# The order around a state-space scan: layer-norm steps one unit earlier, up-projection copies one unit later, one z projection moved

## The chip, the cores and the metric

The kernel runs on one core of a Trainium2 chip. The metric is the device time of one execution in microseconds (us); before the change it is 9294.69 us, the median of three runs that lie between 9293.85 and 9295.26 us.

A core has a matrix engine (PE), a vector engine (DVE), a scalar/activation engine (ACT), a general engine (POOL) and DMA queues, here nearly all fed by SP. Each engine executes its own instructions strictly in the order in which the program gives them; they wait for each other through semaphores.

## The reference: what is computed

The input is a batch of 8 feature maps of 384 channels on 32 x 32 points. Four layers follow each other, each with a group norm in front and a residual around it: a selective state-space layer, a deformable convolution, a second state-space layer with a layer norm ahead of it and a two-layer perceptron (MLP) behind it, and a displaced 5 x 5 convolution. The change touches only the third of them:

```python
def _L2_conv_ref(x, ...):                        # x is already group-normed
    t = x.transpose(0, 2, 3, 1).reshape(b, L, c) # L = 1024 tokens, c = 384
    mu = t.mean(-1, keepdims=True)
    var = t.var(-1, keepdims=True)
    t = (t - mu) * rsqrt(var + 1e-05) * ln_w + ln_b
    xz = t @ in_proj_w.T                         # 384 -> 2 x 768
    xm, z = jnp.split(xz, 2, axis=-1)
    xc = silu(causal_conv3(xm) + conv_b)
    dt, Bm, Cm = split(xc @ x_proj_w.T)
    dt = softplus(dt @ dt_proj_w.T + dt_proj_b)
    # over the 1024 tokens, for 768 channels x 16 states:
    #   h = exp(dt * A) * h + dt * xc * Bm ;  y = sum_n h * Cm
    y = (y + xc * D) * silu(z)
    t = y @ out_proj_w.T
    t = gelu(t @ mlp_w1.T + mlp_b1) @ mlp_w2.T + mlp_b2
```

## The kernel before

`ssm_layer` (called with li = 2 for this layer, where `mlp` is true) cuts the work into 16 steps: 8 samples, each in two halves of 512 tokens. A step has 48 units, written t = 0 to 47: 6 blocks of 128 channels (j) by 8 units (m). A unit is one scan instruction over 128 partitions and 2 x 512 elements. Steps of the first half of a sample are called even here, those of the second half odd. All times quoted for one step are those of step 6 (even) and step 7 (odd).

In a unit each engine has a fixed part, in this order:

- ACT: the unit's entries of the hand-written list `act[t]`, in even steps a tiny copy of the last state (L520), then the two exponentials "decays" (L494) for the scan *two units ahead*, which go into one of two PSUM buffers `da`.
- DVE: the scan (L514); in 5 of 8 units the product with C (`with_c`, L527), which in the other 3 (m = 0, 2, 5) is on POOL (L525); then the list `dve[t]`.
- POOL: the scan's inputs (L502) for three units ahead, into one of three buffers `db`; then `with_c` where it is POOL's; then `pool[t]`.
- PE: the list `pe[t]`, then, in two of 8 units, `read_out` (L537), which sums four units' products into `y` and so frees their `hs` buffers, of which there are seven.

Everything else of a step is put into these lists by `plan`: for step s it places the work of the *next* step's head (norms, in projections `inner`, convolution, x and dt projections), of the present step (z projections and gates), and of the *previous* step's tail (out projection, the MLP's up and down projections). The place in a list alone sets the order on an engine; nothing is rearranged later.

The pieces that matter here, with the line under which the trace shows them:

- the layer norm of the next step: `norm_apply` (ACT, L299), `ln_mean` (PE, L307, into `ps_mu`), `ln_center` (DVE, L312), `ln_square` (ACT, L316), `ln_var` (PE, L321, into `ps_var`), `ln_rstd` (ACT, L326 and L327), `ln_scale` (DVE, L332), `ln_affine` (ACT, L337), and then the first in projection `inner` (PE, L348, unit 16), its copy `conv_last` (ACT, L352) and `conv` (DVE, L368);
- the MLP of the previous step: in each of three rounds q four up projections `mlp_up` (PE, L595), each copied out by `up_take` (ACT, L606), then `gelu` (ACT, L609: a load of ACT's function table and one instruction), `exp_ln` (L377, a table load back), and three down projections (PE, L614) with their sums on DVE (L621, L623);
- the z projection of block 4 (PE, L546) and its gate at unit 31 (ACT, L550, with its own table load);
- of the dt path: `dt_proj` (PE, L408), `soft_exp` (ACT, L414 to L420), `soft_rest` (DVE, L427), `soft_sum` (POOL, L435 to L437), and at the end of a block `close` (DVE, L556 and L557), which reads `y`; `x_store` (ACT, L391) is the copy that dt projections of the next step wait for.

All matrix products named above, except `read_out`, take their PSUM buffer from one pool of three, in turn: the n-th product can start only when the consumer of the (n-3)-rd has read it. In units 8 to 16 the order before is: z0, z1, up 0, up 1, dt projection 3, `ps_mu`, up 2, up 3, `ps_var`, in projection 0.

```python
self.mm = ctx.enter_context(tc.tile_pool(name=f"mm{li}", bufs=3, space=PSUM))
dap = ctx.enter_context(tc.tile_pool(name=f"da{li}", bufs=1, space=PSUM))  # two tags: da0, da1
t = s["hs", m] = p2.tile([P, 2, TS], F32, name="hs", tag="hs", bufs=7)
```

Weights come by DMA ahead of use: a z projection's slice is fetched two units before it (`TZ[j] - 2`), on SP's queue, with three buffers.

Of the kernel before, what the change touches and what calls it, by code (L numbers as in the profile page):

```python
# [96 lines left out]
class Net:  # L97
# [107 lines left out]
    def ssm_layer(self, li, src, dst, shift=None):  # L205
        tc, nc, ins = self.tc, self.nc, self.ins
        mlp = li == 2
# [3 lines left out]
        with ExitStack() as ctx:  # L211
# [435 lines left out]


            TG, TS2 = ((8, 8, 24, 24, 31, 47), (24, 31)) if mlp else ((7, 15, 23, 31, 39, 47), (23, 31))
            TZ = (6, 7, 22, 23, 30, 45) if mlp else tuple(t - 1 for t in TG)  # L650
            TI = (16, 17, 18, 24, 25, 26) if mlp else (15, 16, 17, 24, 25, 26)
            NU = NS // 2
            T = ND * NU
# [1 line left out]
            def plan(prev, s, nxt):  # L655
                act, dve, pool, pe = queues = [[[] for _ in range(T + NU)] for _ in range(4)]

                def put(q, t, fn, *args):
                    if not args or args[0]:
                        q[t].append((fn, *args))  # L660

                for j in range(ND):
                    t = NU * j
                    put(dve, t + 2, close, *((s, j - 1) if j else (prev, ND - 1)))
                    tz = TZ[j]
                    put(pe, tz - 2, fetch_in, s, ND + j)
                    put(pe, tz, z_proj, s, j)
                    put(act, TG[j], gate, s, j)

                    n, k = (s, j + 2) if j + 2 < ND else (nxt, j + 2 - ND)  # L670
                    put(pe, t + 2, dt_proj, n, k)
                    put(act, t + 3, soft_exp, n, k)
                    put(dve, t + 4, soft_rest, n, k)
                    put(act, t + 5, soft_ln, n, k)
                    if pe_sum:
                        put(pe, t + 5, soft_add, n, k)
                        put(act, t + 6, soft_take, n, k)
                        put(dve, t + 7, soft_du, n, k)
                    else:
                        put(pool, t + 6, soft_sum, n, k)  # L680
                    put(pool, t + 7, spread, n, k)
                for i, t in enumerate(TS2):
                    put(act, t, silu, nxt, 3 * i, 3 * i + 3)
                for t in sorted({*TG, *TS2}):
                    put(act, t, exp_ln)
                put(pe, 0, norm_load, nxt)
                if nxt and nxt["h"] == 0:
                    put(dve, 2, norm_stats, nxt, 0)
                    put(dve, 3, norm_stats, nxt, 1)
                    put(dve, 3, lambda n: n.update(gn_mv=self.gn_aggr(n["gn_st"])), nxt)  # L690
                    put(pe, 4, lambda n: n.update(gn_ps=self.gn_mean(n["gn_mv"])), nxt)
                    put(dve, 5, lambda n: n.update(gn_grp=self.gn_dev(n["gn_mv"], n["gn_ps"])), nxt)
                    put(act, 6, lambda n: n.update(gn_dm=self.gn_square(n["gn_grp"][1])), nxt)
                    put(pe, 6, lambda n: n.update(gn_ps=self.gn_mean2(n["gn_dm"])), nxt)
                    put(dve, 8, lambda n: n.update(gn_var=self.gn_sum(n["gn_grp"][0], n["gn_ps"])), nxt)
                    put(act, 9, lambda n: n.update(gn=self.gn_rstd(n["gn_grp"][0], n["gn_var"])), nxt)
                    put(act, 9, lambda n: n["sib"].update(gn=n["gn"]), nxt)
                put(act, 10, norm_apply, nxt)
                if mlp:
                    put(pe, 10, ln_mean, nxt)  # L700
                    put(dve, 12, ln_center, nxt)
                    put(act, 13, ln_square, nxt)
                    put(pe, 13, ln_var, nxt)
                    put(act, 14, ln_rstd, nxt)
                    put(dve, 15, ln_scale, nxt)
                    put(act, 16, ln_affine, nxt)
                for d, t in enumerate(TI):
                    put(pe, t - 2, fetch_in, nxt, d)
                    put(pe, t, inner, nxt, d)
                    put(act, t + 1, conv_last, nxt, d)  # L710
                    put(dve, t + 2, conv, nxt, d)
                put(pe, 32 if mlp else 30, x_proj, nxt, 0, ND // 2)
                put(pe, 33 if mlp else 32, x_proj, nxt, ND // 2, ND)
                put(act, 34 if mlp else 33, x_store, nxt)
                for p, t in enumerate((36, 45)):
                    put(pool, t, load_bc, nxt, p)
                put(act, 7 if mlp else 9, residual, prev)
                for o, (t, e) in enumerate(((0, 2), (1, 3), (4, 5)) if mlp else ((8, 9), (10, 11), (12, 13))):
                    if mlp and o < 2:
                        put(pe, (T - 9, T - 6)[o], fetch, nxt and s, "out", o)  # L720
                    else:
                        put(pe, 0, fetch, prev, "out", o)
                    put(pe, t, out_proj, prev, o, 0, ND // 2)
                    put(pe, e, out_proj, prev, o, ND // 2, ND)
                    put(act if mlp else dve, e + (1 if mlp else 2), out_take, prev, o)
                if mlp:
                    ups = ((8, 9, 11, 12), (27, 28, 29, 31), (37, 38, 39, 40))
                    downs = ((19, 20, 21), (34, 35, 36), (43, 44, 46))
                    for q, g in enumerate((15, 33, 41)):
                        put(pe, (3, 15, 31)[q], fetch, prev, "up", q)  # L730
                        put(pe, (12, 28, 38)[q], fetch, prev, "down", q)
                        for f, t in enumerate(ups[q]):
                            put(pe, t, mlp_up, prev, q, f)
                            put(act, t + 1, up_take, prev, q, f)
                        put(act, g, gelu, prev)
                        put(act, g, exp_ln)
                        for o, t in enumerate(downs[q]):
                            put(pe, t, mlp_down, prev, q, o)
                            put(dve, min(t + 2, T - 1), down_take, prev, q, o)
                return queues  # L740
# [6 lines left out]
            with tc.manual_schedule(engines=ENGINES):  # L747
# [37 lines left out]
                for i, (s, j, m) in enumerate(units):  # L785
                    c, t = divmod(i, T)
                    if t == 0:
                        queues = plan(
                            steps[c - 1] if c else None, s, steps[c + 1] if c + 1 < len(steps) else None
                        )  # L790
                        for k, q in enumerate(over or ()):
                            for i0, items in enumerate(q):
                                queues[k][i0][:0] = items
                        act, dve, pool, pe = queues
                        over = [q[T:] for q in queues]
# [1140 lines left out]
```

## Time and profile before

| | |
|---|---|
| median of the three runs | 9294.69 us |
| the profiled execution | 9297.33 us |
| its span, first to last instruction | 9295.5 us |
| mean granted PE clock | 0.884 |
| even step, first scan to the next step's first scan (steps 2, 4, 6, 8, 10, 12, 14) | 191.3 to 191.4 us |
| odd step (3, 5, 7, 9, 11, 13) | 204.6 us |
| step 0 / step 1 | 199.1 / 199.6 us |

The step lengths are differences between starts of scans (L514) in the trace: step 6 begins at 7026.64 us, step 7 at 7217.99, step 8 at 7422.6. They repeat to about 0.1 us, so one even and one odd step stand for all. A line of the timeline gives start, duration, engine, source line, operation, what is written from what, how many instructions are merged, and in brackets how long the engine was idle before it and which instruction's end let it go. A line of the waits gives the total of such idle time, how often, and the longest. Matrix products in float32 appear as two passes each, so one of three matrix multiplications shows as x6.

### The profile page before, as it was taken

What the parts mean: (1) busy time and instruction counts of PE and PEld (TensorE: products, weight loads), DVE (VectorE), ACT (ScalarE), POOL (GpSimd) and SP (SyncE); (2) the same over time, 40 slices, a digit from 0 to 9 for tenths busy, and PEclk for the clock granted to TensorE, in tenths of its full rate; (3) what the DMA queues carried; (4) which work ended last, traced back from release to release, by engine and by line L of the source; (5) the groups of instructions that cost most, each with busy time, mean ns of one, the idle gap of its engine ahead of it and who ended that gap; (6) DMA issues with size and microseconds to landing.
All of it is one profiled execution on the core that took longest, in us unless ns stands there. A gap on an engine that the chain in (4) does not pass through costs nothing. (4 is left out here: it accounts for less than half of the span.)

```text
span 9295.5 us, 93074 instructions
## 1 busy us (share of the span) xinstructions
PE 7557.6 (81%) x29452; PEld 3856.6 (41%) x29452; DVE 7733.3 (83%) x8617; ACT 6500.3 (70%) x10467; POOL 5645.4 (61%) x3393
## 2 busy tenths in 40 slices
PE   6777677677676999999999997588888888888876
PEld 2222222222223777767777766133333333333333
DVE  6999999999995878878878877788988889898972
ACT  5677677677673878878877876677777677776750
POOL 6999999999994000000000000898989989899964
PEclk7788788788787999999999998798999889999988
DMA  4544544544543333333333333566656666666656
GB/s 123 124 115 113 123 116 114 123 119 114 123 114 81 82 80 85 92 83 85 90 84 86 91 80 85 118 154 151 150 139 155 151 161 147 148 148 145 161 145 112
DMA packets 785233, 1094.47 MB, mean 118 GB/s; under 512 B 274963, under 2 KB 427955, under 8 KB 752985
## 3 DMA queue, kind: packets, MB, share of 16 engines
q1 hardware_dynamic: 722628, 1077.98, 47.6%
q10 hardware_dynamic: 62100, 10.44, 0.7%
q8 instruction: 235, 3.85, 0.2%
q14 instruction: 270, 2.20, 0.1%
HBM read 917.84 MB, written 170.33 MB: 117 GB/s over the span
## 5 line engine op out<-in xcount | busy, mean ns | idle before, releaser
L502 POOL TENSOR_TENSOR db<-dub,bc 128x1024 f32<-128x1024 f32 x1536 | 3603.2, 2355 | 405.9 <-DVE hs L514 224.6
L494 ACT ACTIVATE da<-dtb,vec 128x512 f32<-128x512 f32 x3072 | 2119.5, 691 | 672.9 <-DVE hs L527 416.9
L514 DVE TENSOR_TENSOR_SCAN da<-da,db 128x1024 f32<-128x1024 f32 x912 | 2086.3, 2288 | 258.9 <-ACT da L494 116.4
L435 POOL TENSOR_TENSOR dt<-dt,sp_e 128x512 f32<-128x512 f32 x96 | 122.3, 1274 | 2885.4 <-DMA bc<-bcd 2881.1
L1598 PE MATMUL wacc<-fsm,fxk 128*128 128x221 f32 (+34 forms) x10624 | 1657.2, 315 | 98.1 <-DVE fsm L1568 95.1
L1598 PEld LDWEIGHTS wacc<-fsm,fxk 128*128 128x128 f32 x10624 | 1570.0, 195 | 236.1 <-DVE fsm L1568 159.2
L514 DVE TENSOR_TENSOR_SCAN hs<-da,db 128x1024 f32<-128x1024 f32 x624 | 1423.9, 2282 | 166.4 <-POOL db L487 76.7
L525 POOL TENSOR_TENSOR hs<-hs,bc 128x1024 f32<-128x1024 f32 x624 | 1470.8, 2357 | 15.2 <-ACT st L520 14.9
L1568 DVE TENSOR_TENSOR fsm<-fhy,fhx 128x170 f32<-128x170 f32 (+42 forms) x3216 | 1170.2, 428 | 342.3 <-PE wacc L1598 315.3
L527 DVE TENSOR_TENSOR hs<-da,bc 128x1024 f32<-128x1024 f32 x912 | 1116.9, 1225 | 111.8 <-PE y L537 58.5
L537 PE MATMUL y<-hs,cols 128*32 128x512 f32 x6144 | 826.1, 618 | 160.5 <-POOL hs L525 154.6
L1528 ACT ACTIVATE fhy<-fpyx,cell 128x416 f32<-128x416 f32 (+9 forms) x1280 | 645.5, 576 | 385.0 <-DVE fsm L1568 385.0
L1551 DVE TENSOR_TENSOR fxk<-fxt,fwk 128x1024 f32<-128x1024 f32 (+1 forms) x688 | 787.1, 1179 | 10.2 <-ACT fxt L1330 10.2
L614 PE MATMUL ps_m<-hid,wm 128*128 128x512 f32 x1152 | 550.2, 633 | 61.7 <-ACT hid L609 27.7
L595 PE MATMUL ps_h<-t,wm 128*128 128x512 f32 x1152 | 529.7, 604 | 43.2 <-DVE sp_e L427 25.4
L1533 ACT ACTIVATE fhy<-fhy,cols 128x1344 f32<-128x1344 f32 (+10 forms) x368 | 530.8, 1442 | 12.0
L537 PEld LDWEIGHTS y<-hs,cols 128*32 128x32 f32 x6144 | 171.3, 112 | 798.3 <-issue 497.7
L348 PE MATMUL ps_in<-xn,winr 128*128 128x512 f32 x576 | 328.9, 718 | 174.5 <-ACT xn L337 125.4
L444 PE MATMUL ps_sp<-dt,ident 128*128 128x512 f32 x192 | 168.4, 974 | 290.8 <-ACT dt L414 285.7
L614 PEld LDWEIGHTS ps_m<-hid,wm 128*128 128x128 f32 x1152 | 226.9, 203 | 394.3 <-issue 282.7
L1239 PE MATMUL ps_off<-fxn,fow 128*98 128x465 f32 (+10 forms) x896 | 386.6, 579 | 0.0
L444 PE MATMUL ps_sp<-sp_e,ident 128*128 128x512 f32 x192 | 174.9, 1009 | 259.5 <-DVE sp_e L425 259.5
(212 smaller groups left out, 10436.4 us busy)
## 6 DMA issues: line engine op xcount, KB each, us to landing
dtb<-dtd SPq DMA_DIRECT2D x768, 256.0 KB
dub<-dtd SPq DMA_DIRECT2D x768, 256.0 KB
fpyx<-fposd SPq DMA_DIRECT2D x640, 256.0 KB
wm<-in_w SPq DMA_DIRECT2D x96, 768.0 KB
bc<-bcd SPq DMA_DIRECT2D x256, 256.0 KB
x<-x SPq DMA_DIRECT2D x71, 768.0 KB
dtd<-dt SPq DMA_DIRECT2D x192, 256.0 KB
dtd<-sp_e SPq DMA_DIRECT2D x192, 256.0 KB
```

The source lines that it names most:

```text
L494: nc.scalar.activation(da[:, i, :], s["dtb", j][:, k, :], AF.Exp, scale=na[:, j, n + i : n + i + 1])
L502: nc.gpsimd.tensor_tensor(db, du, s["bc"][p][:, 0], ALU.mult)
L514: nc.vector.tensor_tensor_scan(h1, da1, db1, 0.0, ALU.mult, ALU.add)
L525: nc.gpsimd.tensor_tensor(s["hs", m], s["hs", m], c, ALU.mult)
L527: nc.vector.tensor_tensor(hs_tile(s, m), s["da", m], c, ALU.mult)
L537: nc.tensor.matmul(s["y"][k * IP : (k + 1) * IP, :], sel, s["hs", p * NSUB + k][:, i, :], start=mlp and p == 0 and i == 0, stop=p == NQP - ...
L614: nc.tensor.matmul(ps, s["w2", q][:, f, o * P : (o + 1) * P], s["hid", q][:, f, :], start=(f == 0), stop=(f == 3))
L1528: nc.scalar.activation(hy[:, at : at + (yb - ya) * W], pyx[:, 0, ya * W : yb * W], AF.Abs, bias=bias)
L1533: nc.scalar.activation(hy[:, :at], hy[:, :at], AF.Relu, bias=self.col(Q_ONE), scale=-1.0)
L1551: nc.vector.tensor_tensor(t[:, :n], x, wk[:, j : j + 1, :].to_broadcast([P, n, P]), ALU.mult)
L1568: nc.vector.tensor_tensor(self.sub(sm, at, [(r * w, n), (w, r), (1, w)]), self.sub(hy, hy_at[by] + xa, [(r * W, n), (W, r), (1, w)]), self ...
L1598: nc.tensor.matmul(a[:, ya - 4 * o : yb - 4 * o, xa:xb], k, self.sub(sm, sm_at[by], [(w, yb - ya), (1, w)]), start=False, stop=False,)
```

## The change

Nothing is added or taken away; five kinds of entries change their place in the lists.

- `ln_center` moves from unit 12 to 11, `ln_square` and `ln_var` from 13 to 12, `ln_rstd` from 14 to 13, `ln_scale` from 15 to 14, `ln_affine` from 16 to 15. `norm_apply` and `ln_mean` stay at 10.
- Each `up_take` moves one unit later, but not past the unit of its round's `gelu` (15, 33, 41).
- In round 1 the third up projection moves from unit 29 to 30.
- The z projection of block 4 moves from unit 30 to 29, and its weight fetch from 28 to 27.

```diff
-            TZ = (6, 7, 22, 23, 30, 45) if mlp else tuple(t - 1 for t in TG)
+            TZ = (6, 7, 22, 23, 29, 45) if mlp else tuple(t - 1 for t in TG)
...
                 put(act, 10, norm_apply, nxt)
                 if mlp:
                     put(pe, 10, ln_mean, nxt)
-                    put(dve, 12, ln_center, nxt)
-                    put(act, 13, ln_square, nxt)
-                    put(pe, 13, ln_var, nxt)
-                    put(act, 14, ln_rstd, nxt)
-                    put(dve, 15, ln_scale, nxt)
-                    put(act, 16, ln_affine, nxt)
+                    put(dve, 11, ln_center, nxt)
+                    put(act, 12, ln_square, nxt)
+                    put(pe, 12, ln_var, nxt)
+                    put(act, 13, ln_rstd, nxt)
+                    put(dve, 14, ln_scale, nxt)
+                    put(act, 15, ln_affine, nxt)
...
                 if mlp:
-                    ups = ((8, 9, 11, 12), (27, 28, 29, 31), (37, 38, 39, 40))
+                    ups = ((8, 9, 11, 12), (27, 28, 30, 31), (37, 38, 39, 40))
                     downs = ((19, 20, 21), (34, 35, 36), (43, 44, 46))
                     for q, g in enumerate((15, 33, 41)):
...
                         for f, t in enumerate(ups[q]):
                             put(pe, t, mlp_up, prev, q, f)
-                            put(act, t + 1, up_take, prev, q, f)
+                            put(act, min(t + 2, g), up_take, prev, q, f)
                         put(act, g, gelu, prev)
                         put(act, g, exp_ln)
```

In units 9 to 16 the lists read, before and after:

| unit | before | after |
|---|---|---|
| 9 | ACT: up_take 0 | |
| 10 | ACT: norm_apply, up_take 1. PE: dt projection 3, ln_mean | ACT: norm_apply, up_take 0. PE: the same |
| 11 | ACT: soft_exp 3. PE: up 2 | ACT: soft_exp 3, up_take 1. DVE: ln_center. PE: up 2 |
| 12 | ACT: up_take 2. DVE: soft_rest 3, ln_center. PE: up 3 | ACT: ln_square. DVE: soft_rest 3. PE: ln_var, up 3 |
| 13 | ACT: soft_ln 3, ln_square, up_take 3. PE: ln_var | ACT: soft_ln 3, ln_rstd, up_take 2 |
| 14 | ACT: ln_rstd | ACT: up_take 3. DVE: ln_scale |
| 15 | ACT: gelu, exp_ln. DVE: ln_scale | ACT: ln_affine, gelu, exp_ln |
| 16 | ACT: ln_affine. PE: in projection 0 | PE: in projection 0 |

In round 1 the copies are at units 29, 30, 32, 33 instead of 28, 29, 30, 32, with the gelu at 33; in round 2 at 39, 40, 41, 41 instead of 38, 39, 40, 41, with the gelu at 41.

## The prediction

> **What bounds the kernel now.** First the page.
>
> ```profile
> span 9295.5 us, 93074 instructions
> ...
> PE 7557.6 (81%) x29452; PEld 3856.6 (41%) x29452; DVE 7733.3 (83%) x8617; ACT 6500.3 (70%) x10467; POOL 5645.4 (61%) x3393
> ```
>
> These shares run over four layers. In the stretch from 5800 to 8990 us, the third layer, POOL is busy 2889 of 3190 us, DVE 2780, PE 2605, ACT 2273. No engine is full; what counts is what ends DVE's pauses, since a step is 48 scans in a row. The chain that ended last says nothing here: it covers only the last 180 us, in the fourth layer. So next the waits between 5900 and 8780 us (14 steps).
>
> ```profile
> DVE da L514 <- ACT da L494: 84.3, 47, 2.6
> ...
> DVE y L556 <- PE y L537: 24.4, 14, 2.0
> ...
> ACT hid L606 <- PE ps_h L595: 152.6, 98, 5.1
> ...
> PE ps_in L348 <- ACT xn L337: 121.2, 15, 8.6
> ...
> PE ps_h L595 <- DVE sp_e L427: 25.4, 27, 1.2
> ```
>
> DVE is held by late decays and, once a step, by `y`. ACT's 152.6 us for up projections and PE's 121.2 us for the normed tokens are large, but they cost only what reaches a scan. The last line proves the three-buffer rule: up 3 waits for `soft_rest` 3, the reader of the dt projection three products earlier. Then the timeline of step 6, units 10 to 18, PE first, then ACT, then DVE:
>
> ```profile
> 7062.40 5.49 PE L307 MATMUL ps_mu<-xn,mean_w 128*128 128x512 f32 x6 [2.09 <-ACT xn L299]
> ```
>
> ```profile
> 7075.01 2.84 PE L321 MATMUL ps_var<-sq,mean_w 128*128 128x512 f32 x6 [1.13 <-ACT sq L316]
> 7077.78 1.92 PE L537 MATMUL y<-hs,cols 128*32 128x512 f32 x16
> 7087.71 5.13 PE L348 MATMUL ps_in<-xn,winr 128*128 128x512 f32 x6 [8.01 <-ACT xn L337]
> ```
>
> ```profile
> 7061.55 2.21 ACT L299 ACTIVATE xn<-x,gn_nb,gn_rstd 128x512 f32<-128x512 f32 x3
> 7063.66 0.66 ACT L606 ACTIVATE hid<-ps_h,vec 128x512 f32<-128x512 f32 x1
> ```
>
> ```profile
> 7077.89 0.66 ACT L326 ACTIVATE ps_var<-ps_var,cols 128x512 f32<-128x512 f32 x1 [0.96 <-PE ps_var L321]
> ...
> 7082.09 1.91 ACT L609 ACTIVATE hid<-hid 128x2048 f32<-128x2048 f32 x1
> ...
> 7085.51 1.42 ACT L494 ACTIVATE da<-dtb,vec 128x512 f32<-128x512 f32 x2
> ```
>
> ```profile
> 7065.70 1.22 DVE L527 TENSOR_TENSOR hs<-da,bc 128x1024 f32<-128x1024 f32 x1
> ...
> 7070.90 1.87 DVE L312 TENSOR_TENSOR xn<-xn,ps_mu 128x512 f32<-128x512 f32 x3
> ```
>
> ```profile
> 7087.01 2.30 DVE L514 TENSOR_TENSOR_SCAN da<-da,db 128x1024 f32<-128x1024 f32 x1 [1.07 <-POOL sp_e L437]
> ...
> 7094.79 0.76 DVE L556 SCALAR_TENSOR_TENSOR y<-u,vec,y 128x512 f32<-128x512 f32 x1 [1.94 <-PE y L537]
> ```
>
> To see: `ps_mu` ends at 7067.9, while DVE ends unit 11's product at 7066.9; centring in unit 12 (7070.9) has 3 us to spare. The scan of unit 17 waits 1.07 us; POOL is named, but the decays it needs ended at 7086.93, behind the gelu, so ACT holds it too. `close` waits 1.94 us because PE stood 8.01 us ahead of in projection 0 with `read_out` behind it.
>
> **Part 1: the norm's steps and round 0's copies, even steps.** Today `ps_mu` needs the buffer of up 0, whose copy is in unit 9. The copy moves behind `norm_apply`. `norm_apply` begins 0.65 us earlier (7060.9 to 7063.1), the copy ends at 7063.7, and only then `ps_mu` starts: 7063.75, plus 5.49, is 7069.25. In unit 11 DVE reaches `ln_center` at 7066.92 and waits 2.35 us; behind it stand all later scans. Centring 1.87: the scan of unit 12 starts at 7071.1. From there 4.06 us (7066.84 to 7070.90 today, without centring) to the scan of unit 13: 7075.15 against 7072.69, so +2.45.
>
> `ps_var`, now ahead of up 3, inherits that product's wait for `soft_rest` 3, which ends at about 7075.2. PE has been idle since 7072.1 (up 2 behind `ps_mu`), 3.1 us. Its length is unknown: 2.84 us as in the row after 1.13 us idle, or 5.49 as after 2.09; an in projection after 2.82 idle took 4.32 (at 7132.14), a z projection after 3.50 idle 5.5. I take 4.75, between the last two: end 7079.95. Then on ACT: `ln_rstd` 1.24, copy 0.6, decays for unit 15 1.6 with the state copy: 7083.4; copy 0.6, state copy and first token 0.35, decays for unit 16 1.45: 7085.8; `ln_affine`, now ahead of the gelu, 2.15; gelu with its two table loads 4.5; state copy and decays for unit 17 1.6: 7094.05. Today the scan of unit 17 starts at 7087.01, so +7.0. From it `close` can follow 5.85 us later; today it starts 1.94 after that, which vanishes since in projection 0 starts some 8 us ahead of need. Net **+5.1 us**; with `ps_var` at 2.84 it is +3.2, at 5.49 +5.9. From unit 19 to 25 DVE has no pause that could take this up, and POOL, which idles 3 us for DVE there (unit 21), none either.
>
> The clock: that PE ran `ps_mu` at 0.86 us a pass after 2.09 us idle is the row I go by. [...]
>
> **Odd steps.** `norm_apply` 7267.6 to 7269.8, copy to 7270.4, `ps_mu` 2.84 (PE is warm there, 7270.12 today) to 7273.2; DVE is free at 7272.5, waits 0.7; the scan of unit 13 at 7279.0 against 7278.31. Up 2 waits for its buffer till 7274.8 (`soft_exp` goes ahead of the copy), `ps_var` for `soft_rest` till 7279.1, end 7281.95. Then 1.24 + 0.6 + 1.4 + 0.6 + 1.1 (`first_token` with its four exponentials) + 1.4 + 2.15 + 4.5 + 1.45 lead to 7296.4 against 7292.67: +3.8, less `close`'s wait of 1.52: **+2.3**.
>
> **Part 2: round 1 and the z projection.** From the gate in unit 31 to `x_store` ACT has no pause (7148.51 to 7164.78), and the scans of units 33 and 35 wait for it, 2.40 and 0.97 us. A copy more stands ahead of the gelu (two in units 32 and 33 instead of one): +0.6 us. The 1.26 and 0.33 us that ACT waited in units 29 and 30 vanish, but it waits 0.92 for DVE right after, so nothing is gained. The z projection trades places with up 2 on PE, both 2.8 us; up 3 ends when it did. In odd steps the gate's 0.20 us wait for it goes: +0.4. Its weight fetch meets the same neighbours on SP's queue and the same buffer condition: nothing, and no DMA is added on SP or POOL.
>
> **Part 3: round 2.** Copies leave units 38 and 39, where ACT waited 5.01 and 2.33 us; that frees the decays for unit 41 (its scan waits 1.65). But the gelu in unit 41 needs up 3 of a PE chain without a gap from 7166.84 to 7194.6, ready at 7191.7 as today. The scan of unit 43 stays where it is and waits 4.3 instead of 2.61: 0.
>
> **Sum.** Seven even steps with both neighbours: 7 x (5.1 + 0.6) = 39.9. Seven odd ones (1 to 13, step 1 taken as the rest): 7 x (2.3 + 0.4) = 18.9. Step 15 has only part 2: 0.4. Step 0 has no MLP behind it: the same `ps_mu`, 2.8 us later decays for unit 15, given back where today's product waited 1.26 and `ln_scale` stood in unit 15: 0. In all 59.2 on the profiled 9297.33 us, which lies 2.6 above the median: 9356.5, and **9354** as a median.
>
> **Rivals.**
> - The move does what the waits promise: PE no longer stands before in projection 0, the scan of unit 17 (1.07, odd 1.10) and `close` (1.94, 1.52) no longer wait. With part 2's cost: 7 x (-2.4) + 7 x (-2.2) = -32, 9262. It decides if `ps_mu` ends before DVE's unit 11 product and the decays for unit 17 before unit 16's scan ends. For it: the large PE and ACT waits. Against: `ps_mu` misses even today, by 1.0 us, and `ln_affine` adds 2.15 us in front of the gelu in either step.
> - `ps_mu` is not held by the copy, the buffer being free otherwise: DVE then waits 1.0 instead of 2.35 and PE keeps warm: even +0.5, odd +2.0, with part 2 7 x 1.1 + 7 x 2.4 = 24.5, 9319. Against: the buffers go strictly in turn, as up 3's wait shows.
> - Worse: PE goes cold in odd steps too (1.65 us idle before up 2, where 1.50 was still warm and 2.09 not), `ps_var` 2.6 later: 7 x 6.5 + 7 x 5.3 = 83, 9377.
>
> **Chances.** My forecast 0.66, worse 0.08, the small loss 0.12, the gain 0.10, about nothing (gain and loss cancelling) 0.04. 0.2%, 18.6 us, is about what can be told from no change; the small loss falls just beyond it, with a third of its chance inside. So faster 0.10, same 0.08, slower 0.82. Range 9312 to 9384: from the small loss, which a cheaper `ps_var` (9341) lies above, to the worse case and its own error of a unit's wait.
>
> **What would show it.** A wait DVE L312 on `ps_mu` of about 2.4 us (even) and 0.7 (odd); `ps_mu` starting right after a copy L606; the scan of unit 17 held by ACT by some 5 us; no wait of `close` in unit 18; PE's 8 us ahead of in projection 0 down to about 3; ACT's waits on `ps_h` nearly gone with no gain. I am wrong if `ln_center` does not wait, or if the scan of unit 17 starts less than 2 us later than now.

## The result, and the profile after

| | before | after |
|---|---|---|
| median of 13 runs each, same chip | 9295.25 us (9288.03 to 9300.62) | 9314.15 us (9308.49 to 9317.4) |
| ratio after / before, 95% interval | | 1.002 [1.0013, 1.0028] |
| profiled execution: span | 9295.5 us | 9315.6 us |
| mean granted PE clock | 0.884 | 0.885 |

The change costs 18.9 us. The direction was forecast, the size (59) was three times too large. First the page of the kernel after:

```profile
span 9315.6 us, 93049 instructions
...
PE 7571.2 (81%) x29427; PEld 3863.6 (41%) x29452; DVE 7732.7 (83%) x8617; ACT 6505.8 (70%) x10467; POOL 5648.0 (61%) x3393
```

Nothing was taken away; the 25 PE records fewer than before are matrix products that the trace lacks (the weight loads, PEld, are 29452 in both). DVE, ACT and POOL are busy as long as before to within 6 us, PE 13.6 us longer; DVE's idle time grew by 20.7 us, about the whole difference of the spans. The waits of the kernel after between 5900 and 8780 us (engine, waiting line, what it waited for; total, times, longest), DVE's first:

```profile
DVE da L514 <- ACT da L494: 100.7, 44, 3.5
...
DVE xn L312 <- PE ps_mu L307: 14.0, 13, 1.4
...
DVE y L556 <- PE y L537: 7.4, 13, 0.7
```

```profile
ACT hid L606 <- PE ps_h L595: 32.8, 33, 1.9
```

```profile
PE ps_in L348 <- ACT xn L337: 47.8, 15, 3.5
...
PE ps_mu L307 <- ACT hid L606: 26.9, 14, 3.5
...
PE ps_var L321 <- ACT sq L316: 6.9, 7, 1.0
```

ACT's wait for up projections fell by 120 us and PE's for the normed tokens by 73, and the kernel is slower, so neither wait was what set its time. `ps_mu` now waits for the copy of up 0, DVE for `ps_mu`, and the decays come later. The last line is the one that the prediction did not have: `ps_var` waits for ACT's square, and no wait of it for `soft_rest` 3 (DVE L427) is among PE's waits.

Step 6, which begins 4.16 us later on its trace's own time scale than before (7030.80 against 7026.64). The timelines of the kernel after (start, length, engine, line, tiles; in brackets the idle time ahead and what ended it), PE, then DVE, then ACT:

```profile
7067.97 5.33 PE L307 MATMUL ps_mu<-xn,mean_w 128*128 128x512 f32 x6 [3.51 <-ACT hid L606]
7073.13 2.74 PE L595 MATMUL ps_h<-t,wm 128*128 128x512 f32 x6
7076.85 2.84 PE L321 MATMUL ps_var<-sq,mean_w 128*128 128x512 f32 x6 [0.98 <-ACT sq L316]
...
7087.62 5.49 PE L348 MATMUL ps_in<-xn,winr 128*128 128x512 f32 x6 [3.49 <-ACT xn L337]
```

```profile
7073.40 1.88 DVE L312 TENSOR_TENSOR xn<-xn,ps_mu 128x512 f32<-128x512 f32 x3 [1.12 <-PE ps_mu L307]
...
7078.67 0.68 DVE L427 SCALAR_TENSOR_TENSOR sp_e<-sp_w,ps_dt 128x512 f32<-128x512 f32 x1
...
7095.21 2.30 DVE L514 TENSOR_TENSOR_SCAN da<-da,db 128x1024 f32<-128x1024 f32 x1 [2.69 <-ACT da L494]
...
7100.95 0.73 DVE L556 SCALAR_TENSOR_TENSOR y<-u,vec,y 128x512 f32<-128x512 f32 x1
```

```profile
7067.25 0.67 ACT L606 ACTIVATE hid<-ps_h,vec 128x512 f32<-128x512 f32 x1
...
7080.85 0.64 ACT L326 ACTIVATE ps_var<-ps_var,cols 128x512 f32<-128x512 f32 x1
...
7086.76 2.21 ACT L337 ACTIVATE xn<-xn,vec 128x512 f32<-128x512 f32 x3
7088.99 1.28 ACT L609 ACT_TABLE_LOAD   x1
```

To see: `ps_mu` starts right behind the copy and runs slowly (5.33), as forecast. `ps_var` starts at 7076.85, before `soft_rest` 3 (DVE L427) has even begun at 7078.67, and is warm (2.84 instead of the 4.75 assumed). Its reader on ACT stands at 7080.85 in its place in the list, without a wait. `ln_affine` stands ahead of the gelu, so the scan of unit 17 waits 2.69 us for its decays; `close` (L556) no longer waits.

What does not fit a sum of such waits is the length of the steps. Starts of the first scans of steps 6, 8 and 10:

| kernel | steps 6, 8, 10 start at | two steps | in units of 3.4133 us |
|---|---|---|---|
| before | 7026.64, 7422.56, 7818.49 | 395.92, 395.93 | 115.99, 116.00 |
| after | 7030.80, 7429.99, 7829.41 | 399.19, 399.42 | 116.95, 117.02 |

The unit comes from the granted clock in these traces. It is either 1.00 or 0.50, and every stretch of the one or the other, but for the last of each trace, lasts a whole number of times 3.4133 us; "window" stands for this length here. Stretches of the kernel before (stretch, its length, busy time of PE, PEld, DVE, ACT, POOL with counts, granted clock, DMA share, GB/s), cut at the clock's own changes in step 6:

```profile
7061.62:7068.44 6.82, 6.04 (x7) 2.53 (x8) 6.75 (x6) 6.69 (x13) 6.82 (x4) 0.50 1.07 210
7068.45:7082.10 13.65, 9.89 (x34) 3.31 (x32) 13.48 (x12) 11.30 (x20) 13.65 (x7) 1.00 0.76 215
7082.10:7092.34 10.24, 4.63 (x6) 1.85 (x6) 9.07 (x7) 8.24 (x11) 10.08 (x7) 0.50 0.14 53
7092.34:7133.30 40.96, 36.37 (x117) 13.45 (x116) 36.55 (x31) 31.52 (x62) 35.82 (x18) 1.00 0.63 148
7133.30:7136.71 3.41, 3.16 (x4) 0.68 (x2) 3.34 (x4) 2.70 (x6) 3.41 (x2) 0.50 1.12 224
```

The lengths are 2, 4, 3, 12 and 1 times 3.413 us. In each of the two traces every change of the granted clock after 5900 us, in three thousand us, falls on the same phase of 3.4133 us to within 0.006. So the phase stays the same through all the work of the layer.

### The profile page after: what moved, and what is told of

Its sections match the earlier page's. It is cut to its first block, busy times and chain, and to the rows that moved or that the text cites. A ratio compares the mean times of both kernels' runs of the same rounds, so it can differ in the third digit from the quotient of the medians.

```text
span 9315.6 us, 93049 instructions
## 1 busy us (share of the span) xinstructions
PE 7571.2 (81%) x29427; PEld 3863.6 (41%) x29452; DVE 7732.7 (83%) x8617; ACT 6505.8 (70%) x10467; POOL 5648.0 (61%) x3393
## 5 line engine op out<-in xcount | busy, mean ns | idle before, releaser
L348 PE MATMUL ps_in<-xn,winr 128*128 128x512 f32 x576 | 354.0, 765 | 177.1 <-ACT ps_dt L415 57.9
```

## The experiments

All edits are against the kernel before unless "full" (the change) is said. Medians; the ratio is to the kernel before on the same chip; "pair" is the length of an even and the next odd step in windows of 3.4133 us, from step 4 on.

| run | median us | ratio | pair |
|---|---|---|---|
| e1 norm's six entries alone | 9297.25 | 1.0003 [0.9994, 1.0012] | 115.8 to 116.8 |
| e2 the rest alone (copies, up, z) | 9300.16 | 1.0007 [0.9998, 1.0016] | 116.0 to 116.6 |
| e3 full, first copy ahead of norm | 9307.99 | 1.0013 [1.0004, 1.0022] | 117.0 |
| e4 full, round 0's gelu in unit 16 | 9298.1 | 1.0005 [0.9996, 1.0014] | 115.8 and 117.2 in turn |
| e14 full, e3 and e4 together | 9290.32 | 0.9993 [0.9984, 1.0002] | 115.8 to 116.2 |
| e5 full, `ps_var` behind up 3 | 9340.9 (one run) | none | 118.0 |
| e6 norm alone, gelu in unit 16 | 9291.25 | 0.9995 [0.9986, 1.0004] | 116.0 |
| e7 before, one DVE op a step more | 9294.15 | 0.9999 [0.9989, 1.0008] | 115.8 to 116.2 |
| e8 before, two | 9294.35 | 0.9999 [0.999, 1.0008] | 116.0 to 116.1 |
| e12 before, four | 9338.16 | 1.0042 [1.003, 1.0054] | 117.4 to 118.6, mean 118 |
| e9 full, one | 9308.73 | 1.0014 [1.0005, 1.0024] | 116.9 to 117.1 |
| e10 before, PE kept warm | 9272.66 | 0.9971 [0.9961, 0.9981] | 114.8 to 115.2 |
| e11 e10 and two DVE ops | 9268.12 | 0.9967 [0.9956, 0.9978] | 115.0 to 115.5 |
| e13 e6, PE kept warm | 9269.2 | 0.9968 [0.9957, 0.9979] | 114.8 to 115.1 |
| e15 full, PE kept warm | 9294.11 | 0.9997 [0.9988, 1.0006] | 116.0 to 116.3 |

The lengths are those of one traced execution of each kernel. Added up from step 4 to step 14, five pairs, they fall into groups. The kernel before, e6, e7, e8 and e14 take 1979.7 us, which is 580 windows; the change, e3 and e9 take 1996.8, 585 windows; e5 and e12 take 2013.9 and 2013.8, 590 windows. e1 (1985.8), e2 (1983.2) and e4 (1985.9) lie between the first two groups, and the kernels with PE kept warm lie at 1962.0 to 1981.0.

**The two halves of the change.** e1 has only the six `ln` lines of the change, e2 all the others.

> Only the layer norm's six entries are moved up a unit; copies, third up projection and z projection stay as before. Theory A (the loss sits in the norm's part: ps_mu is held by round 0's first copy, and ln_affine now stands ahead of the gelu on ACT): with the copy back in unit 9, ps_mu starts 1.4 us earlier, DVE's wait at centring falls from 2.3 us (1.1 shown plus 1.2 of a late start) to about 1.0 in even steps and 0.5 in odd ones, but the scan of unit 17 still waits about 2.6 us for the decays behind the gelu; close's 1.9 us wait is gone. Net about +0.5 us a step, 9295 + 7 = 9302 us. Theory B (the loss sits in the copies of rounds 1 and 2, the norm's part is a gain): close's 1.94 and 1.52 us and the scan's 1.1 us are won, 9295 - 30 = 9265 us.

> Only the copies, the third up projection of round 1 and the z projection are moved; the layer norm stays as before. Theory A: ps_mu is held by the copy here too (starts about 1.4 us later in even steps, ends at 42.6 us of the step), but centring in unit 12 comes at 44.3 us, so DVE does not wait; what is left is the copy ahead of round 1's gelu, +0.6 us in even and +0.4 in odd steps: 9295 + 7 = 9302 us. Theory B: all of the loss and more, 9314 us or above.

Neither half alone can be told from the kernel before (+3.1 and +6.0 us by the medians), while together they cost 18.9. Costs that simply add would give 9, but the intervals of the two halves reach up to 11 and 15 us, so the medians alone do not rule out adding. The traces say more: from step 4 to step 14, e1 is 6.0 us longer than the kernel before, e2 3.4, the change 17.0. The split also places the gain in the first two steps: step 0 is 5 us shorter in e1 and after, not in e2.

**Mending the two waits that the change makes.** e3 puts the first copy ahead of `norm_apply`, e4 puts the gelu behind another unit's decays:

```diff
 # e3
+                if mlp:
+                    put(act, 10, up_take, prev, 0, 0)
                 put(act, 10, norm_apply, nxt)
...
-                            put(act, min(t + 2, g), up_take, prev, q, f)
+                            if (q, f) != (0, 0):
+                                put(act, min(t + 2, g), up_take, prev, q, f)
 # e4
-                    for q, g in enumerate((15, 33, 41)):
+                    for q, g in enumerate((16, 33, 41)):
...
-                            put(act, min(t + 2, g), up_take, prev, q, f)
+                            put(act, min(t + 2, g - (q == 0)), up_take, prev, q, f)
```

> The full change, with round 0's first copy placed ahead of norm_apply in unit 10 instead of behind it. Theory A: ps_mu then waits for norm_apply alone; in even steps it starts about 1.4 us earlier relative to the scans, in odd ones about as now (its three products follow norm_apply). 7 x 1.4 = 10 us less than the full change: 9304 us. Theory B: no difference from the full change, 9314 us.

> The full change, with round 0's gelu and the table load behind it in unit 16 instead of 15, so that ln_affine alone stands ahead of the decays for unit 17. Theory A: the scan of unit 17 no longer waits (2.7 us in even, 2.5 in odd steps), that of unit 18 waits about 0.6 instead: 1.9 us a step less, 14 x 1.9 = 26, 9288 us. Theory B: the order around unit 15 is not where the time goes, 9314 us.

> The full change with both repairs: round 0's first copy ahead of norm_apply and round 0's gelu in unit 16. Theory AL (the two conflicts of the norm's part lengthen a pair of steps beyond 116 PE clock windows, and the pair then takes 117): without both, pairs of 116.0 windows, and steps 0 and 1 keep their gain: 9291 us, as the norm alone with the gelu in unit 16. If the copies of rounds 1 and 2 are what takes the pair to 117: 9308 to 9314 us.

e3 alone can't be told from the full change (the intervals overlap, the pair stays at 117.0). In odd steps DVE waits 0.47 us for `ps_mu` instead of 0.95; in even steps `ps_mu` starts 1.4 us earlier but so does DVE, which still waits 1.16. The scan of unit 17 waits for ACT as it does after the change, and in odd steps `ps_var` becomes late instead (ACT waits 1.69 us for it). In e4 the wait does not vanish but moves from unit 17 to unit 18, since the decays for unit 17 need the `da` buffer of unit 15 and the gelu starts only behind them. The timeline of e4, DVE, step 6:

```profile
7079.35 2.27 DVE L514 TENSOR_TENSOR_SCAN da<-da,db 128x1024 f32<-128x1024 f32 x1
7081.73 1.22 DVE L527 TENSOR_TENSOR hs<-da,bc 128x1024 f32<-128x1024 f32 x1
7085.01 2.29 DVE L514 TENSOR_TENSOR_SCAN hs<-da,db 128x1024 f32<-128x1024 f32 x1 [2.06 <-ACT da L494]
7087.22 0.73 DVE L556 SCALAR_TENSOR_TENSOR y<-u,vec,y 128x512 f32<-128x512 f32 x1
```

I had expected 0.6 us there. Both repairs together bring back one whole window per pair (117 to 116), and with the gain of the first two steps the median lies 6 us below that of the kernel before, which the interval does not tell from nothing. The copies of rounds 1 and 2 are moved in e14 as in the change, so they are not what takes the pair to 117. e6, which leaves all copies where they were and has only the norm's entries and the gelu moved, agrees: 9291.25 us and pairs of 116.0, where 9286 was expected, or 9288 to 9291 should pairs be whole windows.

**Who gets a PSUM buffer.** e5 issues `ps_var` behind up 3 instead of ahead of it, with nothing else altered:

```diff
 # e5
-                    put(pe, 12, ln_var, nxt)
...
+                            if (q, f) == (0, 3):
+                                put(pe, 12, ln_var, nxt)
```

> The full change, with ln_var placed behind up 3 in unit 12 instead of ahead of it. Theory C (a PSUM buffer goes to the next product in the order in which its readers stand in the program): up 3 then gets the buffer of ps_mu, free since centring in unit 11, and runs at once; ps_var gets the buffer of dt projection 3 and waits for soft_rest 3, so the line with the wait for DVE sp_e L427 is L321, and ln_rstd on ACT waits about 1.5 us for ps_var. Theory D (buffers go strictly in turn, as my prediction assumed): up 3 is the one that waits for soft_rest 3 (L595 <- DVE sp_e L427) in the full change's order too, ps_var never does.

The waits of e5, PE, 5900 to 8780 us:

```profile
PE ps_var L321 <- DVE sp_e L427: 7.3, 7, 1.0
```

So the three buffers do not go in turn, as the description of the kernel and the prediction have it: in turn, up 3 would get the dt projection's buffer here and `ps_var` that of `ps_mu`. Both orders fit another rule: a new product gets the buffer whose last reader stands earliest in the program. Centring (unit 11) stands ahead of `soft_rest` 3 (unit 12), so the first product after it, here `ps_var`, gets the buffer of `ps_mu`, and the next that of the dt projection. In the kernel before, `soft_rest` 3 stood ahead of centring in unit 12, so that up 3, the first to ask, got the dt projection's buffer by either rule: the one wait that I took for proof could not tell them apart. e5 also costs another whole window: two steps of it take 402.8 us, 118.00 windows.

**Is time lost by the window?** If a pair of steps is held to whole windows, a little more work on DVE, at a place where the scans wait for nobody, must cost nothing, and past a point a whole window. Work without a use (a maximum over a constant tile, into a scratch column) is added in unit 22:

```diff
 # e7: n = 1, e8: n = 2, e12: n = 4; e9: full, n = 1
+                scr = wp.tile([P, 1], F32, name="scr")
...
+            def pad():
+                for _ in range(n):
+                    nc.vector.reduce_max(scr, self.gmat.rearrange("p g c -> p (g c)")[:, :512], axis=AX.X)
...
+                    put(dve, 22, pad)
```

> The kernel before, with one more DVE instruction (a maximum over 128 x 512 of a constant, its result unused) in unit 22 of every step, where no engine keeps DVE waiting. Additive view: about 0.6 us a step by the rows of 128 x 512 on DVE (0.68 us less overlap), 16 x 0.6 = 10: 9304 us, pairs of steps 116.35 windows of 3.413 us long. Theory L: pairs stay at 116.0 windows (9295 us) or go to 117.0 (9319 us), nothing in between that lasts.

> The kernel before, with two such DVE instructions in unit 22 of every step. Additive view: 1.2 us a step, 9314 us, pairs 116.7 windows. Theory L: pairs of 117.0 windows, 9295 + 7 x 3.41 = 9319 us (or 116.0 still, 9295 us).

> The kernel before, with four such DVE instructions in unit 22 of every step (2.4 us a step, 4.8 a pair, which is more than one window of 3.413). Theory L: pairs of 117.0 windows, 9295 + 24 = 9319 us, 9343 if 118. Additive view: 16 x 2.4 = 38 us, 9333 us, pairs of 117.4 windows; with the two instructions' 1.2 us having cost nothing, 9314.

> The full change with one DVE instruction of 0.6 us more in unit 22 of every step. Theory AL: pairs stay at 117.0 windows, 9314 us, since the kernel before took two such instructions a step without a loss. Additive view: 9314 + 10 = 9324 us. If the full change uses up its 117 windows already: 118, 9338 us.

The groups of e8, DVE, show the price of one (busy us and mean ns; then the idle time ahead):

```profile
L658 DVE TENSOR_REDUCE scr<-gmat 128x1 f32<-128x512 f32 x30 | 20.4, 680 | 0.5
```

Two of them, 1.4 us a step by busy time, cost nothing in the end. The traces show where they went. DVE's waits for down projections, 5900 to 8780 us, before and then in e8, whose line numbers are one higher:

```profile
DVE x L623 <- PE ps_m L614: 27.3, 41, 0.9
```

```profile
DVE x L624 <- PE ps_m L615: 5.5, 6, 1.0
```

That is 21.8 us less, about as much as the 20.4 us of added work, though other waits moved too, up and down. Step 6 shows how, in the dt projection just ahead of these products, before and then in e8 (timeline of PE):

```profile
7164.84 2.07 PE L408 MATMUL ps_dt<-dbc,wdt 24*128 24x512 f32 x2 [3.88 <-ACT dbc L391]
```

```profile
7168.84 1.13 PE L409 MATMUL ps_dt<-dbc,wdt 24*128 24x512 f32 x2 [3.88 <-ACT dbc L392]
```

The idle time ahead of it is the same, but in e8 it starts 1.74 us later in the step. Before, half clock had begun at 7164.02, ahead of it; in e8 it begins at 7169.82, when the product is nearly done. A step that came later met a faster clock here, and DVE did not lose the time.

Four cost 42.7 us (9338.16 against 9295.42), about two windows per pair. That is all of their own busy time (16 steps of 2.7 us are 43.5), though the first half of it had been free: had 1.4 us a step stayed absorbed, 22 us would have been left. So the time of e12 alone does not speak for windows, since the additive view gives nearly the same with 0.68 us for one (9339); only its length over five pairs, 590 windows, does. One more on top of the change also costs nothing: 117 windows on average, 9308.73.

**Taking the slow stretches away.** Products of two constants, into a buffer that the following product overwrites, keep PE busy through three of its gaps:

```diff
 # e10, e11 (n = 9), e13, e15 (n = 4)
+            def warm(ps, n):
+                for _ in range(n):
+                    nc.tensor.matmul(ps, mean_w, self.gmat.rearrange("p g c -> p (g c)")[:, :512], start=True, stop=True)
...
+                if mlp and d == 0 and s is not steps[0]:
+                    warm(ps, n)
...
+                if mlp and j == 0 and s is not steps[0]:
+                    warm(ps, 3)
...
+                if (q, o) == (2, 1) and s is not steps[-1]:
+                    warm(ps, 3)
```

They stand ahead of in projection 0, of the first dt projection and of the second down projection of round 2.

> The kernel before, with products of constants added on PE where it otherwise idles for 3 us or more and then runs slowly: nine ahead of in projection 0, three ahead of the dt projection of block 0, three ahead of the second down projection of round 2, each into the buffer that the real product overwrites afterwards. Theory L (a pair of steps is pulled to whole PE clock windows because the slow stretches end only at a window's edge, and they are on the path that sets the scans): with most slow stretches gone, close's wait of 1.9 and 1.5 us, the 0.6 to 0.8 us at unit 36 and the 0.7 to 0.9 at unit 47 shrink, and a pair need no longer be a whole number of windows: up to 6 us a pair less, 9295 - 7 x 6 = 9253, at the least 9295. The view that the clock does not matter: more PE work in otherwise idle time, no difference, 9295 us with pairs of 116.0 windows.

> The same, plus two DVE instructions of 0.6 us each in unit 22 of every step, which cost the kernel before nothing. Theory L: with the slow stretches gone they are no longer absorbed and cost what they take, 16 x 1.2 = 19 us over the warm kernel without them. If they still cost nothing, slow stretches that are left (the odd steps' waits for weights, ps_mu) do the pulling, or theory L is wrong about the cause.

> The layer norm's entries moved up and round 0's gelu in unit 16 (9291 us alone, pairs of 116.0 windows), with the same products of constants, four instead of nine ahead of in projection 0. Theory L: freed of whole windows, a pair loses what the moves win and what the slow stretches cost, 2 to 6 us: 9291 - 7 x 4 = 9263 us. If the clock does not matter: 9291 us.

> The full change with products of constants that keep PE from slowing down (four ahead of in projection 0, three ahead of the dt projection of block 0, three ahead of the second down projection of round 2). Theory AL: the slow stretches hold this kernel too, so it falls by about as much as the kernel before did (23 us): one window a pair, 9290 us, and stays about one window a pair above the kernel before with its warm products (9273). If the whole loss is only a matter of where the slow stretches fall, it ends with the other, at 9273 us or below.

Half clock from step 6 to step 12 falls from 221.9 us before to 119.5 in e10, by ten windows per pair, and the pair gets one window shorter: nearly half of the slow time was covered. The gain is less than expected in e10 (9272.66 against 9253). The two DVE operations of e11 are absorbed again, against the expectation that with PE warm they would cost 19 us. The slow stretches that are left may still hold the length, or the windows are not the cause there; no run separates the two. e13 is no faster than e10 (9263 was expected). The change on a warmed kernel (e15) takes 116.0 to 116.3 windows per pair against some 115 in e10, and 21 us more, but the two were timed apart, each against the kernel before, and e15 has four products ahead of in projection 0 where e10 has nine. So e15 shows only roughly that the loss stays. e10, e11 and e13 take 0.29 to 0.33% less than the kernel before.

## Why the prediction was right or wrong

- **`ps_mu` behind the copy: right.** In step 6 copy, start and length (5.33 us) are as forecast. DVE waits 1.12 instead of 2.35, because DVE itself now comes 1.2 us later into this unit; the scan of unit 13 is late by 2.42 (forecast 2.45). In odd step 7 it is late by 2.27 (forecast 0.7); DVE waits 0.95 there and was 1.24 late before.
- **"`ps_var`, now ahead of up 3, inherits that product's wait for `soft_rest` 3": the step that failed.** Its ground, that buffers go strictly in turn, is wrong, as e5 shows. `ps_var` started when ACT's square was ready (7076.85, before `soft_rest` 3 began at 7078.67), after 0.98 us idle it took 2.84 us and not 4.75, and `ln_rstd` did not wait. The forecast put the even step 5.1 us behind, the trace has 1.98 from unit 19 on: 3.1 us in each of seven steps, 22 of the 40 us by which the forecast was too high.
- **`ln_affine` ahead of the gelu: right in kind.** With `ps_var` in time, the scan of unit 17 is late by 4.04 instead of 7.0, 2.69 of it a wait for decays; e4 and e14 confirm this cause, since moving the gelu changes that wait's place and, with the copy mended too, ends the loss. `close`'s wait of 1.94 is gone as said. From unit 19 on odd step 7 is 2.06 us behind (forecast 2.3), of which 1.24 was there in unit 8 already.
- **Round 1 and round 2: right in their own terms.** The wait of the scan of unit 35 went from 0.97 to 1.57 us, +0.6. In round 2 the 1.65 us at unit 41 left, and the scan of unit 43 took it over (3.54 instead of 2.61, and 0.72 in `close`), net 0. The forecast lacks two others: in unit 36 of step 6 DVE waits 0.98 instead of 0.56 for a down projection, and at the step's end it no longer waits 0.69 for another.
- **Step 0 at 0 and step 1 "as the rest": wrong.** They are 5.1 and 2.1 us shorter. The norm's earlier end lets the in projections free the three weight buffers sooner, so the fetches come sooner: in projections waited 11.6 us for them in this layer before and not at all after. The timeline of PE in step 0, before and then after (the layer's first scan starts 5.1 us later on the time scale of after):

```profile
5937.59 5.03 PE L348 MATMUL ps_in<-xn,winr 128*128 128x512 f32 x6 [6.07 <-DMA winr<-in_win]
...
5949.17 4.36 PE L348 MATMUL ps_in<-xn,winr 128*128 128x512 f32 x6 [5.50 <-DMA winr<-in_win]
```

```profile
5937.30 2.84 PE L348 MATMUL ps_in<-xn,winr 128*128 128x512 f32 x6 [1.65 <-ACT sz L550]
...
5947.22 4.20 PE L348 MATMUL ps_in<-xn,winr 128*128 128x512 f32 x6 [6.03 <-ACT st L520]
```

- **The sum, 7 x even + 7 x odd: its form was wrong.** Per step the change nets +2.3 us in even and about +1.1 in odd steps, 3.4 a pair, which is one window. Over steps 2 to 14 the steps are 22.2 us longer; the first two give back 7.2, and 5.1 of the span's 20.1 lie ahead of this layer, where the two kernels do not differ: over all kernels the first scan in it spreads from 5835 to 5842. In the traces the two halves of the change (e1 and e2) do not add up to it, so no sum of separate terms could be relied on, this one with better terms neither.
- **The rival "small loss"** came nearest (9319), but not for its own reason, since `ps_mu` was held by the copy, and by luck: its +0.5 and +2.0 us a step, without part 2, met +2.3 and +1.1 in all.
- **Two slips of the prediction that do not matter.** 7296.4 less 7292.67 is 3.7, not 3.8. "1.50 was still warm" has no row in the trace of this layer: the nearest, after 1.43 us at 7307.95, was warm (3.67 us for eight passes), while a product after 1.51 us in the fourth layer (9080.18) took 5.49 us.

**What stays open.** That the steps of this loop hold to whole windows is shown by the lengths, in ten of the seventeen kernels over five pairs to within 0.03 of a window, and by the added work that costs nothing. Why is in the main argued: PE's half-clock stretches begin and end at a window's edge (the same phase of 3.4133 us throughout, in both traces), and some of them lie ahead of a wait of DVE, so a step that arrives a little later can find the same edge or, as in e8, a faster product. Only that one place was followed. Which stretch holds which pair was not separated, and e1, e2, e4 and the warmed kernels do not settle on whole numbers.

## What to carry to other kernels

Before costing a moved wait, find out which buffer the moved instruction really gets: read who stands first as last reader in the program's order, and look for that wait in the trace, since one observed wait proves only the pair that it was seen on. In a loop whose PE switches its clock, as here between 1.00 and 0.50 in stretches of whole multiples of 3.4133 us, compare the length of an iteration with that length first: here a pair of steps was 116.0 of them, the two halves of the change showed next to nothing one by one (+3.1 and +6.0 us), and together they cost a whole window per pair. What went below the kernel before beyond doubt here was filling PE's idle gaps (0.29 to 0.33%, e10, e11, e13). Large waits of an engine that is early (here 120 us of ACT's) are no promise of any gain.

## What the runs showed of the hardware

The same idle time was followed by different lengths: the z projection of block 5, after 3.31 us idle in odd step 7, took 5.49 us before and 2.84 after (timeline of PE):

```profile
7410.76 5.49 PE L546 MATMUL ps_z<-xn,winr 128*128 128x512 f32 x6 [3.31 <-DVE sp_e L427]
```

```profile
7419.15 2.84 PE L546 MATMUL ps_z<-xn,winr 128*128 128x512 f32 x6 [3.31 <-DVE sp_e L427]
```

So no single length of an idle gap decides here: half clock followed 3.31 us in one and not in the other, while `ps_mu` before ran slowly (5.49 us) after 2.09 us. Nor does the time that PE was busy in the window just ahead decide alone. These are the windows ahead of the z projection before, of the z projection after, and of `ps_mu` before (columns as in the views of windows above):

```profile
7406.37:7409.78 3.41, 1.08 (x3) 0.19 (x1) 3.38 (x3) 1.71 (x3) 3.41 (x2) 1.00 0.60 117
```

```profile
7414.33:7417.74 3.41, 1.51 (x4) 0.38 (x2) 3.38 (x3) 2.12 (x4) 3.41 (x2) 1.00 0.87 171
```

```profile
7058.21:7061.62 3.41, 2.10 (x5) 0.48 (x3) 1.97 (x2) 3.31 (x7) 3.41 (x2) 1.00 0.94 278
```

PE was busy for 1.08, 1.51 and 2.10 us in them. Half clock followed the first and the third, not the second. PE had work in all three, so half clock did not need a window without any. What sets the clock was not found.
